# A recurrence stage re-divided between four engines and the transfer queues: |A|² and a running sum by accumulating transfers, one spectrum made twice, stores on another queue, a new order

## The chip, the cores and the metric

The kernel runs on one core of a Trainium2 chip. The metric is the device time of the whole program in microseconds (us), the median over runs. The core has a matrix engine (PE), a vector engine (DVE), a scalar engine (ACT), a general engine (POOL, GpSimd) and a queue engine (SP, SyncE). Each executes its own list of instructions strictly in order and waits at semaphores for the others. Transfers (DMA) are issued from SP (page queue q1) and from POOL (q0).

## The reference

Four layers on an image of 256×256 pixels with 128 channels. The change lies in layer 1 and at its seam to layer 2, so only layer 1 is shown (`x_ri` is the group-normalised image, 64 real and 64 imaginary channels; the result is added to the image).

```python
forget_gate = sigmoid(x_ri @ Wf + bf + 2.0)
input_gate = sigmoid(x_ri @ Wi + bi)
delta = softplus(x_ri @ Wd + bd) * 0.1
A_f = fft2 of the padded 7x7 kernels A (complex);  B_f likewise
mag = sqrt(Ar ** 2 + Ai ** 2 + 1e-08)
scale = 0.95 * sigmoid(mag) / (mag + 1e-08)
Ar, Ai = Ar * scale, Ai * scale
Bx_r, Bx_i = Br * x_r - Bi_ * x_i, Br * x_i + Bi_ * x_r
inp = delta * input_gate * Bx                 # real and imaginary part
# 16 times, from h = 0:
#   Ah = A * h (complex);  h_r = fg_r * Ah_r + inp_r;  h_i = fg_i * Ah_i + inp_i
```

Layer 2 begins with a group normalisation of the new image, so it needs that image's sum and sum of squares by channel. Layer 3 needs nine 128×128 products of its taps with a dense weight; they depend on no data.

## The kernel before

The program runs layer after layer; the image goes through DRAM between them (`x1T` into the recurrence, `x2T` out of it). `recurrence` (L864 to L1117) works on 64 blocks of 1024 pixels. A block's tiles hold 128 partitions (64 channels by two halves of the pixels) and, for each of real and imaginary, 512 numbers: a "wide" tile has 128×1024 numbers, a "thin" one 128×512. The 16 recurrence steps are done in closed form: with the 2×2 matrix of a step, its trace (tile `t`) and determinant (`d`), the 16th power is reached by repeated squaring.

The steps of a block are small functions of two or three letters (L994 to L1092), each one or a few instructions on one engine. The tuple `order` (L1095) lists each with a lag: in iteration `it`, step `(s, k)` works on block `it - k`, so five blocks are in flight. Everything is pinned to this order (`keep_in_program_order`), apart from the loads; so each engine's instructions follow the tuple, and each engine waits only where its next instruction does. There are 68 iterations (64 blocks and the largest lag, 4).

The steps that matter here, by engine:

- PE writes results into PSUM. `za`, `zb` are the spectra of A and B (14-row products of the tables `hs` and `ev`), `zd`, `zf`, `zi` the three gates, `bx` and `av` complex products by sums over identity-like matrices (L982), `m2` the sum |A|² of two squares, `pxb` a sum of three terms (step `xb`). The tiles tagged "z" (`za`, `zb` and the gates) share two PSUM buffers: a new one waits until the reader of the one before last is done.
- ACT: `a2` squares `za`, `zaa` copies both parts of `za` to the tile `ar` in SBUF; `lm`, `mg`, `lb`, `iv`, `sg` form the scale out of |A|²; `ab`, `ae`, `al_` belong to the softplus; `ig`, `f` are the gates' sigmoids; `tq*`, `dn*` squarings; `lD`, `eD` a reciprocal; `ev_` and `bn` (L1085, L1086) make the sum and the sum of squares of the result, with `accum_out` into `parts`. Changes between the logarithm's and the sigmoid's table are two table loads per iteration.
- DVE: products and sums of tiles: `s`, `fs_`, `ff`, `d_`, `D_`, `p0`, `p1` (spectrum B times image, tile `p`), `q`, `qg`, `v`, `tr*`, `u4`, `u8`, `xa`, `be`, `e_`, `al`, `y0`, `y1` (A's spectrum `ar` times `v`, tile `y`), `yf`, `yb`.
- POOL: `pf` (tile `fs`), `t`, `u2` (tile `u`), `t1` (tile `t` from `t,v`), and its queue: `ac1` and `ac2` add two results to the image tile `xc` by accumulating transfers (512 KB each), and `st` stores `xc` in two halves (L1091).
- SP: the loads of a block (`load`, L931): `xf` 512 KB, `xc` two of 256 KB, `hs` eight of 3.5 KB.

At the stage's end PE is kept warm (56 products), DVE reduces `parts`, and `triangle` (L1119) begins with `tap_products` (L1488: ten products of PE, four copies of DVE) and `group_affine` (L83), which reduces the statistics again, averages them by groups on PE, and forms scale and shift.

Of the kernel before, what the change touches and what calls it, by code (L numbers as in the profile page):

```python
# [9 lines left out]
F32 = mybir.dt.float32  # L10
# [21 lines left out]
class Kernel:  # L32
# [50 lines left out]
    def group_affine(self, pool, psum, stats, tag, shift=None, mv=None, busy=8):  # L83

        nc, V = self.nc, self.nc.vector
        pin = self.tc.keep_in_program_order
        pm = psum.tile([P, 2], F32, name=f"pm{tag}", tag="gn")
        d, v, mg, sd = (pool.tile([P, 1], F32, name=f"{n}{tag}") for n in ("gd", "gv", "mg", "sd"))
        if mv is None:
            mv = pool.tile([P, 2], F32, name=f"mv{tag}")  # L90
            V.tensor_reduce(mv, stats, AX.X, ALU.add)
            self.keep_busy(psum, busy)
            pin(self.mm(pm, self.g4n, mv))
            self.keep_busy(psum, 3)
            V.tensor_tensor(d, pm[:, 0:1], shift, ALU.add)
            V.scalar_tensor_tensor(v, d, d, pm[:, 1:2], ALU.mult, ALU.subtract)
            V.tensor_copy(mg, pm[:, 0:1])
            self.chain("table", self.act(sd, v, AF.Sqrt, bias=self.eps, scale=-1.0))
        else:
            self.keep_busy(psum, busy)  # L100
            pin(self.mm(pm[:, 0:1], self.g4, mv[:, 0:1]))
            self.keep_busy(psum, 3)
            V.tensor_copy(mg, pm[:, 0:1])
            V.tensor_sub(d, mv[:, 0:1], mg)
            V.scalar_tensor_tensor(v, d, d, mv[:, 1:2], ALU.mult, ALU.add)
            pv = psum.tile([P, 2], F32, name=f"pv{tag}", tag="gn")
            pin(self.mm(pv[:, 0:1], self.g4, v))
            self.keep_busy(psum, 3)
            self.chain("table", self.act(sd, pv[:, 0:1], AF.Sqrt, bias=self.eps))
        ab = pool.tile([P, 2], F32, name=f"ab{tag}")  # L110
        V.reciprocal(ab[:, 0:1], sd)  # L111
        V.scalar_tensor_tensor(ab[:, 1:2], mg, -1.0, ab[:, 0:1], ALU.mult, ALU.mult)
        return ab, mg, sd
# [750 lines left out]
    def recurrence(self, x1T, x2T, HD_, stats1, shift1, stats2, shift2):  # L864
# [7 lines left out]
        with ExitStack() as c:  # L872
# [40 lines left out]
            parts = wp.tile([P, 2, 2, NB], F32, name="parts2")  # L913
            shiftc = wp.tile([P, 2], F32, name="shiftc")
            V.tensor_copy(shiftc, abc[:, :, 1])
            fold = wp.tile([P, HC], F32, name="fold")
            V.tensor_tensor(fold, self.ident[:, :HC], self.ident[:, HC:], ADD)
            rows = lambda t: t.rearrange("p i (r v) -> p r i v", v=N)
# [5 lines left out]
            def act(out, in_, func, **kw):  # L924
                want = tables.get(func)
                if want not in (None, current[0]):
                    pin(nc.scalar.preload_act_table_set(want))
                    current[0] = want
                return pin(self.act(out, in_, func, **kw))

            def load(b):  # L931
                d = D[b]
                xf = d["xf"] = io.tile([P, 1024], F32, name="xf", bufs=2)
                nc.sync.dma_start(xf, x1T[:, b * 1024:(b + 1) * 1024])
                xc = d["xc"] = io.tile([P, 2, 512], F32, name="xc", bufs=6)
                for half in range(2):
                    src = x1T[:, b * 1024 + half * 512:b * 1024 + (half + 1) * 512]
                    nc.sync.dma_start(xc[half * HC:(half + 1) * HC], src.rearrange("(r c) n -> c r n", c=HC))
                d["hs"] = self.first_rows if b == 0 else self.row_transforms(io.tile([P, 2, HC], F32, name="hs", bufs=2), HD_, b)
# [3 lines left out]
            def wide(d, n, bufs=1):  # L943
                d[n] = tp.tile([P, 2, 512], F32, name=n, tag="w" + n, bufs=bufs)
                return d[n]
# [28 lines left out]
            def total(d, name, pairs):  # L974

                n = len(pairs)
                z = d[name] = ps.tile([P, n, 512], F32, name=name, tag="y" if n == 2 else "s", bufs=1 if n == 2 else 2)
                for i, terms in enumerate(pairs):
                    for k, (m, t) in enumerate(terms):
                        pin(self.mm(z[:, i], m, t, start=k == 0, stop=k == len(terms) - 1))  # L980
# [14 lines left out]
            def a2(d): act(rows(wide(d, "a2")), d["za"], AF.Square)  # L995
            def m2(d): total(d, "m2", [[(self.ident, d["a2"][:, 0]), (self.ident, d["a2"][:, 1])]])
            def lm(d): act(thin(d, "mag"), d["m2"][:, 0], AF.Ln, bias=1e-8)
# [5 lines left out]
            def ab(d): halves(d, wide(d, "az"), "d", "zd", AF.Identity)  # L1003
            def ae(d): act(wide(d, "ex"), d["az"], AF.Sigmoid, scale=-1.0)
            def al_(d): act(d["ex"], d["ex"], AF.Ln, bias=1e-37)
            def q(d): stt(wide(d, "q", 2), d["ex"], -1.0, d["az"], MUL, MAX)

            def sg(d): act(d["mag"], d["mag"], AF.Sigmoid)
            def s(d): tt(thin(d, "s", 3), d["mag"], d["inv"], MUL)
# [3 lines left out]
            def ig(d): halves(d, wide(d, "ig"), "i", "zi", AF.Sigmoid)  # L1013
            def zaa(d): act(wide(d, "ar", 2), d["za"].rearrange("p r i v -> p i r v"), AF.Copy)
# [3 lines left out]
            def t(d): gt(thin(d, "t", 3), d["fs"], d["ar"][:, 0], MUL)  # L1018
            def d_(d): tt(thin(d, "d"), d["m2"][:, 0], d["ff"], MUL)
# [20 lines left out]
            def dn2(d): squared(d, "dn2", "d", 2)  # L1040
            def tr2(d): stt(thin(d, "tr2"), d["d"], -2.0, d["tq2"], MUL, ADD)
            def u2(d): gt(thin(d, "u2", 2), d["t"], d["tr2"], MUL)
# [3 lines left out]
            def u4(d): tt(thin(d, "u4"), d["u2"], d["tr4"], MUL)  # L1046
            def tq8(d): squared(d, "tq8", "tr4")
            def dn8(d): squared(d, "dn8", "dn4", 2)
# [3 lines left out]
            def xa(d): stt(thin(d, "g", 2), d["t"], -2.0, d["u8"], ADD, MUL)  # L1052
# [13 lines left out]
            def y0(d): tt(wide(d, "y0"), d["ar"], both(d["v"][:, 0]), MUL)  # L1066
            def y1(d): tt(wide(d, "y1"), d["ar"], both(d["v"][:, 1]), MUL)
            def av(d): real_and_imaginary(d, "av", d["y0"], d["y1"])
            def yf(d): tt(wide(d, "yf", 2), d["av"], d["f"], MUL)
            def t1(d): (tt if last(d) else gt)(wide(d, "t1"), both(d["t"]), d["v"], MUL)  # L1070
# [14 lines left out]
            def ev_(d): statistic(d, 0, AF.Identity)  # L1085
            def bn(d): statistic(d, 1, AF.Square, shifted=True)  # L1086
            def st(d):
                b = d["b"]
                for half in range(2):
                    dst = x2T[:, b * 1024 + half * 512:b * 1024 + (half + 1) * 512]  # L1090
                    pin(nc.gpsimd.dma_start(dst.rearrange("(r c) n -> c r n", c=HC), d["xc"][half * HC:(half + 1) * HC]))  # L1091
            def ld(d): load(d["b"])  # L1092
# [3 lines left out]
                (e_, 3), (ld, 0), (za, 0), (u4, 2), (zb, 1), (a2, 0), (av, 2), (t, 1), (p1, 1), (zaa, 0), (m2, 0),  # L1096
                (tq8, 2), (al, 3), (zd, 0), (ev_, 4), (lD, 2), (q, 1), (yf, 2), (p0, 1), (tq2, 1), (dn2, 1), (tr2, 1),
                (eD, 2), (tr8, 2), (lm, 0), (dn8, 2), (mg, 0), (ab, 0), (t1, 3), (qg, 1), (lb, 0), (tq16, 2), (bx, 1),
                (ac1, 3), (iv, 0), (u8, 2), (yb, 3), (zf, 0), (sg, 0), (tq4, 1), (v, 1), (y1, 1), (f, 0), (xa, 2),
                (D_, 1), (s, 0), (u2, 1), (ac2, 3), (tr4, 1), (ae, 0), (fs_, 0), (zi, 0), (y0, 1), (ff, 0), (pf, 0),  # L1100
                (xb, 2), (ig, 0), (be, 2), (al_, 0), (bn, 4), (d_, 0), (dn4, 1), (st, 4),
            )
            deep = max(lag for _, lag in order)
            for it in range(NB + deep):
                for step, lag in order:
                    if 0 <= it - lag < NB:
                        D[it - lag]["b"] = it - lag
                        step(D[it - lag])
            warm = ps.tile([P, 1, 512], F32, name="warm", tag="s")
            for _ in range(56):  # L1110
                pin(self.mm(warm[:, 0, :P], self.ident, self.cmat))
            red = wp.tile([P, 2, 2], F32, name="partsum")
            V.tensor_reduce(red, parts, AX.X, ADD)
            pr = ps.tile([P, 2], F32, name="partps", tag="s")
            for ri in range(2):
                self.mm(pr[ri * HC:(ri + 1) * HC], fold, red[:, :, ri])
            V.tensor_copy(stats2[:, :, 0], pr)  # L1117

    def triangle(self, x2T, x3T, znT, prodD, rs2D, rs3D, stats2, shift2, stats3, shift3, prepare):  # L1119
# [12 lines left out]
        with ExitStack() as c:  # L1132
            wp = c.enter_context(self.pool(name="tw", bufs=1))
            with self.pool(name="twp", bufs=2, space=PSUM) as ps0:
                self.tap_products(ps0)
                ab, mg, _ = self.group_affine(wp, ps0, stats2, "2", shift=shift2, busy=0)
# [351 lines left out]
    def tap_products(self, ps):  # L1488

        W, V = self.weights, self.nc.vector  # L1490
        kt, wd = W["kt"], W["wd"]
        pb = ps.tile([P, 2], F32, name="cpb", tag="gn")
        self.mm(pb[:, 0:1], wd, W["bv"])
        V.tensor_copy(W["bw"], pb[:, 0:1])
        for t in range(3):
            pk = ps.tile([P, 3, P], F32, name="cpk")
            for n in range(3):
                self.mm(pk[:, n], kt[:, 3 * t + n, :], wd)
            V.tensor_copy(kt[:, 3 * t:3 * t + 3, :], pk)
# [178 lines left out]
    def run(self, ctx):  # L1678
# [10 lines left out]
        stats["2"] = const.tile([P, 2, 1], F32, name="stats2")  # L1689
        shift2 = const.tile([P, 1], F32, name="shift2")  # L1690
# [87 lines left out]
```

## Time and profile before

| what | value |
|---|---|
| median of 3 runs | 4687.53 us (4685.58 to 4689.0) |
| profiled execution, device time | 4687.51 us |
| its span, first to last instruction | 4685.7 us, granted PE clock 0.992 |
| recurrence: first `za` to the reduction of `parts` | 1654.5 to 2982.4 us |
| busy in 1700 to 2900 us | DVE 1192.3, ACT 1189.6, PE 1133.7, POOL 827.3 of 1200 us |
| DMA engines' share in the same stretch | 0.56 |
| first product of the next stage on the image (`mn`) | 2990.0 us |

The span is 1.8 us shorter than the device time. In the stage all compute engines are nearly always busy. An instruction's duration overlaps the next one's start by some 0.08 to 0.1 us on DVE and ACT, so sums of durations exceed the time; a step's price on its engine is the distance from its start to the next start. Busy time of PE is modelled, and POOL's includes time in which it holds an instruction that makes no progress.

### The profile page before, as it was taken

Reading aid. Unit: us, or ns where it says so; the run is one execution under the profiler, and the core shown is the slowest. Engines: PE = TensorE matmul, PEld = TensorE weight load, DVE = VectorE, ACT = ScalarE, POOL = GpSimd, SP = SyncE. Lnnn points to the kernel's source line nnn. Section 1 sums busy time; section 2 is a strip of 40 time slices with the busy share of each in tenths; the row PEclk is TensorE's granted clock in tenths of the full one; section 3 lists DMA queues with packets and bytes.
Section 4 is the critical chain, followed back from the end, with each engine's and each line's share of the span. In section 5 each row is a group of like instructions: output and inputs, shape, how many; then the busy total and the mean of one; then the engine's idle time right before and its main releaser. Section 6 shows DMA issues by size and latency. Waiting matters only on the chain. (4 is left out here: it accounts for less than half of the span.)

```text
span 4685.7 us, 79549 instructions
## 1 busy us (share of the span) xinstructions
PE 4524.4 (97%) x30447; PEld 2603.2 (56%) x30447; DVE 3753.2 (80%) x4828; ACT 3329.8 (71%) x5173; POOL 2099.7 (45%) x1364
## 2 busy tenths in 40 slices
PE   8999999999999989999999999899999999999999
PEld 2444555555555533333333333456999973379999
DVE  6776777777777779999999999787666677789885
ACT  6555888888888889999999999698443454442210
POOL 0343555555555547666667676333231245520000
PEclk9999999999999999999999999999999999999999
DMA  8894122222222235555555555576667668955432
GB/s 308 299 351 148 46 82 82 85 88 82 86 82 82 78 85 134 132 136 129 131 132 132 134 130 126 175 253 250 240 218 268 247 212 328 357 214 174 135 114 72
DMA packets 221045, 768.12 MB, mean 164 GB/s; under 512 B 58831, under 2 KB 62181, under 8 KB 180317
## 3 DMA queue, kind: packets, MB, share of 16 engines
q1 hardware_dynamic: 154550, 465.37, 29.2%
q0 software_dynamic: 64752, 297.22, 22.0%
q8 instruction: 244, 4.00, 0.3%
q14 instruction: 139, 1.13, 0.1%
q10 hardware_dynamic: 1360, 0.40, 0.0%
HBM read 431.26 MB, written 265.55 MB: 149 GB/s over the span
## 5 line engine op out<-in xcount | busy, mean ns | idle before, releaser
L586 DVE TENSOR_TENSOR e<-sc,bT 128x1024 f32<-128x1024 f32 x512 | 613.5, 1219 | 255.3 <-PE sc L61 254.2
L586 POOL TENSOR_TENSOR ks<-e 128x1024 f32<-128x1024 f32 x256 | 602.0, 2372 | 442.7 <-PE nd L61 429.3
L55 ACT ACTIVATE e<-e 128x1024 f32<-128x1024 f32 x512 | 539.4, 1054 | 39.2 <-DVE e L586 29.6
L61 PE MATMUL m<-U,v 128*128 128x128 f32 x4608 | 514.8, 275 | 1.5 <-DVE v L1613 1.5
L61 PEld LDWEIGHTS m<-U,v 128*128 128x128 f32 x4608 | 514.6, 192 | 1.6 <-DVE v L1613 1.6
L61 PEld LDWEIGHTS z<-wf,zt 128*128 128x128 f32 x4096 | 462.6, 192 | 54.2 <-DVE LR L1126 28.7
L61 PE MATMUL z<-wf,zt 128*128 128x128 f32 x4096 | 474.8, 277 | 6.2 <-DVE LR L1126 6.2
L1126 DVE TENSOR_TENSOR LR<-z,sg 128x512 f32<-128x512 f32 (+1 forms) x323 | 269.9, 866 | 165.4 <-ACT sg L55 165.4
L1126 POOL TENSOR_TENSOR zt<-zt,df 128x512 f32<-128x512 f32 x127 | 161.2, 1270 | 423.4 <-ACT df L55 423.4
L55 ACT ACTIVATE sg<-z 128x512 f32<-128x512 f32 (+1 forms) x323 | 160.7, 509 | 244.3 <-PE z L61 242.0
L61 PE MATMUL sc<-proj 32*128 32x256 f32 x4096 | 300.2, 404 | 2.9 <-DVE e L586 1.9
L955 POOL TENSOR_TENSOR fs<-f 128x512 f32<-128x512 f32 x64 | 174.5, 2727 | 273.7 <-DVE f L952 253.9
L61 PEld LDWEIGHTS sc<-proj 32*128 32x128 f32 x4096 | 188.4, 186 | 160.4 <-PE px L61 94.7
L61 PE MATMUL nd<-e,proj 128*32 128x256 f32 x4096 | 272.3, 384 | 2.6 <-DVE og L586 2.6
L55 ACT ACTIVATE dn<-dn 128x512 f32<-128x512 f32 x384 | 238.0, 620 | 10.2 <-DVE dn L586 6.1
L955 POOL TENSOR_TENSOR u<-t,tr 128x512 f32<-128x512 f32 x64 | 237.0, 3704 | 10.9 <-DVE tr L958 9.8
L955 POOL TENSOR_TENSOR t<-t,v 128x1024 f32<-128x1024 f32 x63 | 206.8, 3282 | 60.7 <-DVE t L952 60.7
L1653 ACT COPY m4s<-m 128x512 f32<-128x512 f32 x32 | 18.7, 585 | 301.4 <-PE m L61 301.4
L61 PE MATMUL z<-LR 128*128 128x256 f32 x1024 | 225.5, 384 | 7.5 <-DVE LR L1126 7.5
L1663 POOL DMA_DIRECT2D out_dram<-ys x32 | 36.9, 1155 | 420.3 <-DVE ys L1661 420.3
L61 PEld LDWEIGHTS z<-LR 128*128 128x128 f32 x1024 | 197.0, 193 | 35.1 <-DVE LR L1126 8.3
L1126 POOL TENSOR_TENSOR zt<-ga,zt 128x1024 f32<-128x1024 f32 x62 | 144.7, 2351 | 117.5 <-DVE ga L1126 117.5
(420 smaller groups left out, 10744.2 us busy)
## 6 DMA issues: line engine op xcount, KB each, us to landing
zt<-znT SPq DMA_DIRECT2D x96, 1024.0 KB
zt<-x2T SPq DMA_DIRECT2D x64, 1024.0 KB
xin<-in_x_dram SPq DMA_DIRECT2D x48, 1024.0 KB
xr<-x3T SPq DMA_DIRECT2D x46, 768.0 KB
x1T<-x POOLq DMA_DIRECT2D x64, 512.0 KB, 5.0
xf<-x1T SPq DMA_DIRECT2D x64, 512.0 KB
xc<-x1T SPq DMA_DIRECT2D x128, 256.0 KB
x2T<-xc POOLq DMA_DIRECT2D x128, 256.0 KB, 3.6
```

The lines of the kernel that those rows point to most:

```text
L55: return self.nc.scalar.activation(out, in_, func, bias=bias, scale=scale, **kw)
L61: return self.nc.tensor.matmul(out, lhsT, rhs, start=start, stop=stop)
L586: pin = lambda f: lambda *a, **k: tc.keep_in_program_order(f(*a, **k))
L955: pin(nc.gpsimd.tensor_tensor(out, a, b_, op))
L1126: pin = lambda f: lambda *a, **k: tc.keep_in_program_order(f(*a, **k))
L1653: nc.scalar.copy(m4, m[4])
L1663: nc.gpsimd.dma_start(out[row:row + 8].rearrange("r p t c -> p (r t) c"), ys.rearrange("p g k t c -> p (g k t) c"))
```

## The change

- `m2`: the two PE products are gone; an accumulating transfer on POOL's queue adds the second half of tile `a2` to the first (256 KB). Its readers, `lm` and `d_`, read `a2` in SBUF instead of PSUM.
- `ev_`: except for the last block, ACT's two passes with accumulation are gone; an accumulating transfer on POOL's queue adds `xc` to a tile `summed` (512 KB), which DVE reduces once at the end.
- `zaa` copies the real part alone. `y0`, `y1` read A's spectrum from PSUM, where a new step `zc` (lag 2, two products of PE) makes it again; it takes a "z" buffer, and `hs` gets three buffers.
- `u4` moves from DVE to POOL. `t1` of the last block moves from DVE to POOL.
- `st` moves from POOL's queue to SP's, pinned; in the program it stands between the fourth and the fifth `hs` load of the next block.
- The tuple `order` is new, and some tiles' buffer counts change.
- `tap_products` leaves `triangle` and is pinned at the head of iteration 2 of the recurrence, with its PSUM tiles under the tag "s" (two buffers).
- The group means are formed at the stage's end by products with `folded`; `group_affine` takes them as `means`.

```diff
-    def group_affine(self, pool, psum, stats, tag, shift=None, mv=None, busy=8):
+    def group_affine(self, pool, psum, stats, tag, shift=None, mv=None, busy=8, means=None):
...
+            else:
+                pm = means
...
+            V.memset(parts, 0.0)
+            summed = io.tile([P, 2, 512], F32, name="summed", bufs=1)
+            nc.gpsimd.memset(summed, 0.0)
...
+            folded = wp.tile([P, HC], F32, name="folded")
+            V.tensor_tensor(folded, self.g4n[:, :HC], self.g4n[:, HC:], ADD)
...
-            def m2(d): total(d, "m2", [[(self.ident, d["a2"][:, 0]), (self.ident, d["a2"][:, 1])]])
-            def lm(d): act(thin(d, "mag"), d["m2"][:, 0], AF.Ln, bias=1e-8)
+            def m2(d): pin(nc.gpsimd.dma_start(d["a2"][:, 0], d["a2"][:, 1], accum_op=ADD))
+            def lm(d): act(thin(d, "mag"), d["a2"][:, 0], AF.Ln, bias=1e-8)
...
-            def zaa(d): act(wide(d, "ar", 2), d["za"].rearrange("p r i v -> p i r v"), AF.Copy)
+            def zaa(d): act(thin(d, "ar", 2).rearrange("p (r v) -> p r v", v=N), d["za"][:, :, 0], AF.Copy)
...
-            def d_(d): tt(thin(d, "d"), d["m2"][:, 0], d["ff"], MUL)
+            def d_(d): tt(thin(d, "d"), d["a2"][:, 0], d["ff"], MUL)
...
-            def u4(d): tt(thin(d, "u4"), d["u2"], d["tr4"], MUL)
+            def u4(d): gt(thin(d, "u4"), d["u2"], d["tr4"], MUL)
...
-            def y0(d): tt(wide(d, "y0"), d["ar"], both(d["v"][:, 0]), MUL)
-            def y1(d): tt(wide(d, "y1"), d["ar"], both(d["v"][:, 1]), MUL)
+            def zc(d): spectrum(d, 0, "zc")
+            def turned(d, n, k):
+                v = d["v"][:, k].rearrange("p (r v) -> p r v", v=N).unsqueeze(2).to_broadcast([P, 2, 2, N])
+                tt(rows(wide(d, n)), d["zc"], v, MUL)
+            def y0(d): turned(d, "y0", 0)
+            def y1(d): turned(d, "y1", 1)
...
-            def t1(d): (tt if last(d) else gt)(wide(d, "t1"), both(d["t"]), d["v"], MUL)
+            def t1(d): gt(wide(d, "t1"), both(d["t"]), d["v"], MUL)
...
+                if last(d):
+                    statistic(d, 0, AF.Identity)
+                else:
+                    pin(nc.gpsimd.dma_start(summed, d["xc"], accum_op=ADD))
...
-                    pin(nc.gpsimd.dma_start(dst.rearrange("(r c) n -> c r n", c=HC), d["xc"][half * HC:(half + 1) * HC]))
+                    pin(nc.sync.dma_start(dst.rearrange("(r c) n -> c r n", c=HC), d["xc"][half * HC:(half + 1) * HC]))
...
+                (ld, 0), (za, 0), (a2, 0), (zc, 2), (m2, 0), (bx, 2), (zaa, 0), (ac2, 4), (u2, 2), (dn8, 3), (pf, 1),
+                (v, 2), (tq16, 3), (xb, 3), (t, 1), (tq4, 2), (y1, 2), (zd, 0), (ae, 1), (dn2, 2), (y0, 2), (lD, 2),
+                (ab, 0), (be, 3), (zb, 1), (ff, 1), (eD, 2), (av, 2), (tq2, 1), (lm, 0), (mg, 0), (e_, 3), (tr4, 2),
+                (al, 3), (zi, 0), (p0, 1), (dn4, 2), (lb, 0), (p1, 1), (al_, 1), (iv, 0), (u4, 2), (yf, 2), (ig, 0),
+                (t1, 3), (d_, 1), (tq8, 2), (yb, 3), (zf, 0), (tr2, 1), (q, 1), (f, 0), (tr8, 2), (qg, 1), (ac1, 3),
+                (u8, 2), (sg, 0), (s, 0), (D_, 1), (bn, 4), (xa, 2), (ev_, 4), (st, 4), (fs_, 0),
...
+                if it == 2:
+                    self.tap_products(ps)
...
+            V.tensor_reduce(parts[:, 0, :, 0:1], summed, AX.X, ADD)
```

## The prediction

> **What bounds the kernel now.** I read the busy times of the stage's middle first, then where one step, `v`, starts in each block, then each engine's timeline over one iteration, last the seam to the next stage.
>
> The windows view (columns: stretch, length, busy us and instructions of PE, weight load, DVE, ACT, POOL, then clock, DMA share, GB/s) shows DVE and ACT at 99%:
>
> ```profile
> 2000.00:2400.00 400.00, 378.34 (x1148) 132.76 (x1148) 396.51 (x495) 396.23 (x671) 270.68 (x159) 1.00 0.56 131
> ```
>
> The instructions around tile `bx` give the step `v`: count, shortest/median/longest ns, first and last start. 63 distances in 1268.6 us: 20.14 us per iteration.
>
> ```profile
> L958 DVE SCALAR_TENSOR_TENSOR v<-q,bx x64: 1204/1215/1222, 1684.1 to 2952.7; 128x1024 f32<-128x1024 f32 x64
> ```
>
> DVE's timeline (start, duration): two of three iterations take 19.65 us from `v` to `v`, which is DVE's own work; about each third takes 21.15. In the long ones `qg` lasts 2.31 instead of 1.22. Start to start, a 128x512 step costs 0.60 (112.29 to 112.89, leaving out the 2000), a 128x1024 one 1.14, two `p` 1.32.
>
> ```profile
> 2098.86 2.31 DVE L952 TENSOR_TENSOR q<-q,ig 128x1024 f32<-128x1024 f32 x1
> ...
> 2112.29 0.68 DVE L952 TENSOR_TENSOR u<-u,tr 128x512 f32<-128x512 f32 x1
> 2112.89 1.40 DVE L958 SCALAR_TENSOR_TENSOR p<-xc,abc,zb 128x512 f32<-128x512 f32 x2
> 2114.21 0.69 DVE L952 TENSOR_TENSOR t<-u,t 128x512 f32<-128x512 f32 x1
> ```
>
> POOL's timeline: the same 128x512 product takes 1.31 beside `p` and 4.49 beside a run of other DVE steps. Its 4.49 end 1.2 us after DVE turns to `v` at 2122.47, a step with one operand in PSUM. So POOL computes only while DVE reads PSUM: 1.22 to 1.3 us for 512 numbers, 2.33 for 1024. The transfer's distance to the next instruction, 0.63, is what issuing one costs.
>
> ```profile
> 2119.20 4.49 POOL L955 TENSOR_TENSOR u<-t,tr 128x512 f32<-128x512 f32 x1
> 2128.58 2.79 POOL L955 TENSOR_TENSOR fs<-f 128x512 f32<-128x512 f32 x1 [3.20 <-DVE f L952]
> 2132.61 1.31 POOL L955 TENSOR_TENSOR t<-fs,ar 128x512 f32<-128x512 f32 x1
> 2134.62 3.31 POOL L955 TENSOR_TENSOR t<-t,v 128x1024 f32<-128x1024 f32 x1 [0.70 <-DVE t L952]
> 2138.23 0.94 POOL L1077 DMA_DIRECT2D xc<-t  x1 [0.30 <-POOL t L955]
> 2138.86 4.48 POOL L955 TENSOR_TENSOR u<-t,tr 128x512 f32<-128x512 f32 x1
> ```
>
> PE's timeline; the distances are its prices: `pxb` 2.77, `zb` before `av` 1.13, `m2` 1.91, `zd` 1.87 (1.94 with its tail), `bx` 3.63.
>
> ```profile
> 2145.25 1.13 PE L61 MATMUL pxb<-g,ident 128*128 128x512 f32 x2
> ...
> 2148.02 1.13 PE L61 MATMUL za<-ev,hs 14*128 14x512 f32 x4
> 2148.94 1.20 PE L61 MATMUL zb<-ev,hs 14*128 14x512 f32 x4
> 2150.07 1.13 PE L61 MATMUL av<-y,ident 128*128 128x512 f32 x2
> ...
> 2154.29 1.98 PE L61 MATMUL m<-a,ident 128*128 128x512 f32 x4 [0.52 <-ACT a L55]
> 2156.20 1.94 PE L61 MATMUL zd<-xf,gwd 128*64 128x512 f32 x8
> 2158.07 1.13 PE L61 MATMUL bx<-p,scaledr 128*128 128x512 f32 x2
> ...
> 2161.70 1.94 PE L61 MATMUL zf<-xf,gwf 128*64 128x512 f32 x8
> ```
>
> **The parts, per iteration.** *DVE* loses `u4`, 0.60. `y0`, `y1` now read PSUM; `yf`, which does so already, costs 1.14 like them: 0, at worst 2 x (1.32 - 1.14) = 0.36 if they go like `p`. `d_` reads SBUF: 0.60 as before. DVE: 19.65 - 0.60 = 19.05 (to 19.41).
>
> *ACT* loses `ev_` (two of 0.63 and two reads of 0.19: 1.37 from its first start at 2115.26 to `D` at 2116.63) and half of `zaa` (0.91 to 0.52): 19.8 - 1.76 = 18.0. *PE* loses `m2`, 1.91, and gains `zc`, 1.13; `za` and `zb` (2169.17, both in 1.1) no longer overlap: about 19.0. *POOL* gains `u4` (1.25), two transfers to issue (0.63 each, the distance after `ac1`), loses two stores (1.30).
>
> *POOL's windows.* In DVE's new order PSUM readers stand together: `v`, `y1`, `y0`, `be` (4.02) and `p0`, `p1`, `yf` (3.8). POOL's queue puts `u2`, `pf`, `t` (3 x 1.25 = 3.75) before the first gap and `u4`, `t1` (1.25 + 2.33 = 3.58) in the second window. They fit, with 0.3 and 0.2 to spare, so I price `u4` on POOL at nothing. If a window is missed, a DVE step waits as `qg` does (1.1), or POOL waits as in the 4.49 row (3.2).
>
> [...]
>
> *A new ring of waits.* `zc` takes the "z" buffer of `zf` and waits until ACT has finished `f`. PE then goes `zc` 1.13, `bx` 3.63, `pxb` 2.77, `zd` 1.94 in order: 9.47, with two hand-overs (0.06, 0.08 as at the first `za`) 9.61. ACT's `ab` waits for `zd`, and from `ab` to the end of `f` ACT has (starts to starts): `ab` 1.14, six of 0.52 (`eD`, `tq2`, `lm`, `mg`, `dn4`, `lb`), 0.14 because `mg` directly follows `lm` that feeds it (0.66 in the `inv` pair at 1664.62), `al_` 0.97, `iv` 0.62, table 1.30, `ig` 1.13, `tq8` 0.52, `f` 1.25: 10.19. The ring is 9.61 + 10.19 = 19.80 us, and it must be gone round once per iteration. It exceeds DVE's 19.05 and ACT's 18.0. ACT idles at `ab`, 1.2 us, for it. So the period falls from 20.14 to 19.80, not to 19.05. [...] Bounds: 19.6 (without the 0.14 and the hand-overs) to 20.0.
>
> *Where the rest lies in it*, counted from the end of `f`: `sg`, `bn`, `a2` end at 0.4 + 1.55 + 1.0 = 3.0; `bx` ends at 4.8, so `v` starts at 4.9; `zd` ends at 9.5, `zb` and `av` (3.70) at 14.4, `zi` and `zf` (1.78, 1.94) at 18.1. DVE from `v`: 4.02, then `ff`, `e_`, `tr4`, `al` (2.4), `p0`, `p1` (2.64): 14.0, so `yf` waits 0.45 for `av`, and DVE's round is 19.5.
>
> *Transfers.* `m2` is issued at 3.1, and `lm`, with all of ACT behind it, wants it at 9.6 + 1.14 + 1.04 = 11.8. The nearest rows are accumulations of 512 KB: 4.4 to 7.2 us to landing, median 4.9. Half the bytes can't need more than 7.2, so 1.5 is left: cost 0, and no gain, since it sets no end. `ev_` (512 KB, same row) is waited for only by the next one and the end. A 512 KB accumulation keeps the DMA engines busy some 2.7 us (share near 1 from 2138 to 2142), so 4 us are added per 19.8: 0.56 becomes about 0.77. Behind `m2` on POOL stand `ac2` and `u2`; `ac2` goes out at 3.7, `u2` wants its window at 4.7. On SP the two stores (0.65 each) wait for `ac2` to land, and behind them stand four `hs` (0.83 each), then `xf` and `xc`. `za` of the next block needs those `hs`. PE reaches `za` at 18.1 and can bear 18.9 (19.8 less `za`'s 0.92). With 6.3 for `ac2` (4.9 and half a transfer of 2.7 in front), 3.7 + 6.3 + 1.3 + 3.3 = 14.6, and some 2.5 to land (below the least landing seen, 3.0 for 256 KB): 17.1. Covered, with 1.8 to spare.
>
> *Filling, draining, seam.* `v` of block 0 moves from iteration 1 to 2. I lay the steps on end with the durations of the first rows: `a2` ends at 1657.4, `m2` lands 4.9 later, then `lm`, `mg`, `lb`, `iv` (2.6), table 1.3, `ig`, `f`, `sg` (2.9): 1669.0. Second round: `a2`, `zaa`, `ae`, `ab` to 1672.6, `tq2` to 1675.1 (POOL's `pf` and `t` need 2.6 from `p0` at 1671.8), table, `lm` to `iv` (3.5 with `al_`), table, `ig`, `f`: 1683.5. So `zc` could start at 1683.6 and `v` at 1688.4, against 1684.07. But the taps' copies are pinned on DVE behind `fs_` (ends 1686.7), and with two "s" buffers the second and third group of products wait for copies: `za`, in order behind them, starts at about 1688.9, `v` at 1694.6. So the fill costs 10.5 us, 6.2 of it the taps; bounds 4 and 13. The first distance shrinks to about 17 (no `pxb`), from 18.0. Draining: after the last `v`, before, 29.2 us; now ACT has two passes less after DVE's end (3.0), but the chain `ac1`, `ac2`, `ev_` of block 62 (4.9 each) stands beside it: about 25.4. Seam: without taps and the second reduction `mn` could start 4.5 us earlier, but the 1 MB `zt` it reads is loaded from 2983.5 at 410 GB/s and can't be there before about 2988, so 2.0. The memsets and `folded` lie in idle time of POOL and DVE.
>
> Sum: last `v` at 1694.6 + 17 + 62 x 19.80 = 2939.2, 13.5 before the old 2952.7; draining -3.8; seam -2.0: **-19.3 us**. On the profiled execution's 4687.51, which the median (4687.53) matches, that is 4668.2.
>
> **The rivals.**
> 1. DVE sets the pace (the ring is shorter than its terms): DVE's round of 19.5: 62 x 0.3 less, 4649.6. For it: DVE is what bounds now; against: PE's and ACT's terms are plain rows. 0.12.
> 2. No change: POOL's windows slip in some iterations as now, 0.49 on average; the ring hides 0.2 of it in DVE's slack: period 20.1, 4687. For it: 0.2 to 0.3 us of room, and the same pattern in the old order; against: POOL reaches each window early. 0.17.
> 3. Slower: the stores on SP. If `ac2` needs over 8.1 us to land (18.9 less the terms above), each further us delays `za`, `zc` and so the period. With 9.3 the period is 21.0: 4668 + 62 x 1.2 = 4743; with 8.5, 4693. For it: the longest landing now is 7.2, and `m2` is put in front, `ev_` beside; against: the median leaves 1.8. 0.16.
>
> **How the numbers follow.** Forecast 0.55 (4655 to 4681 by the ring's bounds, with some 6 either way from the fill), rivals 0.12, 0.17, 0.16. The range, 4648 to 4700, leaves out most of rival 3 above (0.14) and little below (0.05). Of this kernel a measurement can tell about 0.2%, 9.4 us, from no change. Faster: 0.47 of the forecast and rival 1, 0.59; the same: 0.08 of the forecast and 0.12 of rival 2, 0.20; slower: the other 0.05 of rival 2 and rival 3, 0.21.
>
> **What would show it.** Right: `v` every 19.8 us without long iterations; ACT waiting about 1.2 us at `az` for `zd`; PE waiting at `zc` for `f`; `qg` always near 1.22; no wait at `mag` for the transfer. Wrong: DVE idle at `ff` or `qg` with POOL's `u` beside it (rival 2); `za` waiting for `hs`, SP waiting long for `xc<-yf` (rival 3); DVE without a wait at `v` (rival 1); in the fill, `v` of block 0 earlier than 1690.

## The result, and the profile after

The changed kernel takes 4787.17 us (median of 4 runs, 4785.01 to 4787.85) against 4688.26 for the kernel before on the same chip: a ratio of 1.0212, 95% interval 1.02 to 1.0225. It is 2% slower, some 99 us, where the prediction said 4668.2.

The profiled execution has a span of 4783.2 us (before 4685.7) and a granted PE clock of 0.964 (before 0.992). The windows view of the same stretch as before (length, then busy us and instructions of PE, weight load, DVE, ACT, POOL, then clock, DMA share, GB/s) shows where to look:

```profile
2000.00:2400.00 400.00, 383.62 (x1085) 133.20 (x1082) 357.03 (x451) 346.30 (x562) 208.75 (x166) 0.91 0.76 159
```

DVE and ACT, 99% busy before, are now busy for 89% and 87% of the time. PE is busy for longer with fewer instructions, and its granted clock is 0.91 instead of 1.00. The transfers' share rose to 0.76, as estimated (0.77).

The instructions around tile `bx` give `v` (count, shortest, median and longest ns, first and last start):

```profile
L966 DVE SCALAR_TENSOR_TENSOR v<-q,bx x64: 1207/1221/1223, 1699.4 to 3044.4; 128x1024 f32<-128x1024 f32 x64
```

63 distances in 1345.0 us are 21.35 us per round, against 20.14 before and 19.80 forecast. PE's timeline of one round and the start of the next (start, duration, product, count, and in brackets the idle time before it and what ended it) shows what a round holds:

```profile
2199.45 1.89 PE L61 MATMUL zf<-xf,gwf 128*64 128x512 f32 x8
2201.72 1.20 PE L61 MATMUL za<-ev,hs 14*128 14x512 f32 x4 [0.38 <-ACT ig L55]
2203.40 1.95 PE L61 MATMUL zc<-ev,hs 14*128 14x512 f32 x4 [0.48 <-ACT f L55]
2205.28 2.08 PE L61 MATMUL bx<-p,scaledr 128*128 128x512 f32 x2
2207.15 1.92 PE L61 MATMUL bx<-p,scaledn 128*128 128x512 f32 x2
2208.85 1.79 PE L61 MATMUL bx<-p,scaledi 128*128 128x512 f32 x2
2210.48 1.02 PE L61 MATMUL bx<-p,scaledr 128*128 128x512 f32 x2
2211.34 1.02 PE L61 MATMUL pxb<-g,ident 128*128 128x512 f32 x2
...
2224.61 1.20 PE L61 MATMUL za<-ev,hs 14*128 14x512 f32 x4 [0.39 <-ACT ig L55]
2226.28 1.13 PE L61 MATMUL zc<-ev,hs 14*128 14x512 f32 x4 [0.48 <-ACT f L55]
2227.34 1.98 PE L61 MATMUL bx<-p,scaledr 128*128 128x512 f32 x2
```

PE waits at `za` for `ig` and at `zc` for `f`, as the ring of waits says. But then the same products last almost twice as long: `zc` 1.95 instead of 1.13, a pair of `bx` 1.92 instead of 1.02, and then 1.02 again. `bx` takes 6.06 us here and 3.63 before. That is the clock at half. The trace has a record of the granted clock; in this round it falls to half at 2203.57 and is back at 2210.40. The windows view, cut at these times and in steps of 3.41 us (columns as above):

```profile
2200.16:2203.57 3.41, 2.55 (x12) 0.69 (x10) 3.41 (x5) 3.40 (x7) 0.72 (x1) 1.00 0.98 171
2203.57:2206.98 3.41, 3.41 (x6) 1.04 (x7) 3.41 (x6) 3.38 (x8) 0.37 (x1) 0.50 1.00 233
2206.98:2210.40 3.42, 3.42 (x5) 1.35 (x4) 0.88 (x1) 3.40 (x6) 2.48 (x4) 0.50 0.80 158
2210.40:2213.81 3.41, 3.41 (x9) 1.33 (x7) 2.16 (x2) 1.35 (x2) 2.63 (x3) 1.00 1.04 227
```

DVE and ACT pay for it:

```profile
2206.65 1.22 DVE L960 TENSOR_TENSOR f<-f,s 128x1024 f32<-128x1024 f32 x1
2211.61 1.22 DVE L966 SCALAR_TENSOR_TENSOR v<-q,bx 128x1024 f32<-128x1024 f32 x1 [3.75 <-PE bx L61]
2212.87 2.35 DVE L960 TENSOR_TENSOR y<-zc,v 128x1024 f32<-128x1024 f32 x2
```

The starts of `za` from 1836 to 2890 us are 19.53 us apart 6 times, 21.2 apart 28 times and 22.9 apart 15 times. By the record of the clock the 6 have no stretch at half clock, the 28 have one of 3.41 us and the 15 one of 6.83. So a round is 19.53 at full clock, 1.7 more with 3.41 us at half clock (half of it) and 3.35 more with 6.83. Had all rounds been of 19.53, the 63 distances would have taken 1230.4: the clock costs 114.6 us, more than the whole loss of 99.

### The profile page after: what moved, and what is told of

Its sections match the earlier page's. It is cut to its first block, busy times and chain, and to the rows that moved or that the text cites. A ratio compares the mean times of both kernels' runs of the same rounds, so it can differ in the third digit from the quotient of the medians.

```text
span 4783.2 us, 79487 instructions
## 1 busy us (share of the span) xinstructions
PE 4632.4 (97%) x30449; PEld 2633.6 (55%) x30449; DVE 3698.1 (77%) x4766; ACT 3234.8 (68%) x4921; POOL 1945.7 (41%) x1429
## 3 DMA queue, kind: packets, MB, share of 16 engines
q14 instruction: 138, 1.13, 0.1%
## 5 line engine op out<-in xcount | busy, mean ns | idle before, releaser
L55 ACT ACTIVATE dn<-dn 128x512 f32<-128x512 f32 x384 | 238.6, 621 | 10.1 <-DVE dn L589 6.0
L963 POOL TENSOR_TENSOR u<-u,tr 128x512 f32<-128x512 f32 x64 | 105.8, 1654 | 264.9 <-DVE tr L966 264.9
L1004 POOL DMA_DIRECT2D a<-a x64 | 54.6, 853 | 386.9 <-ACT a L55 386.9
L55 ACT ACTIVATE az<-zd,gbd 128x512 f32<-128x512 f32 x128 | 81.0, 684 | 183.5 <-PE zd L61 181.3
L966 DVE SCALAR_TENSOR_TENSOR v<-q,bx 128x1024 f32<-128x1024 f32 x64 | 78.1, 1221 | 151.6 <-PE bx L61 151.6
```

Source lines behind the costliest of these rows:

```text
L55: return self.nc.scalar.activation(out, in_, func, bias=bias, scale=scale, **kw)
L963: pin(nc.gpsimd.tensor_tensor(out, a, b_, op))
L966: pin(V.scalar_tensor_tensor(out, a, k, b_, op0, op1))
L1004: def m2(d): pin(nc.gpsimd.dma_start(d["a2"][:, 0], d["a2"][:, 1], accum_op=ADD))
```

## The experiments

The first theory: the new order puts two products of 14 rows, with a short wait before each, between the last gate and `bx`; PE does too little there, and its clock is halved. Rivals: the waits alone do it (a); the few rows alone do it (b); the taps' products or the fill start it (c). All times are medians, all ratios against the kernel before in the same batch. A period is the mean distance of `v`, as above.

### zc behind bx

```diff
-  (za, 0), (a2, 0), (zc, 2), (m2, 0), (bx, 2), (zaa, 0),
+  (za, 0), (a2, 0), (m2, 0), (bx, 2), (zc, 2), (zaa, 0),
```

> Only the step zc moves, from in front of bx to behind it; nothing else changes. Theory (the ring f, zc, bx, pxb, zd, ab, f sets the period, and PE's clock falls because PE waits between zf, za and zc, where it has only two 14-row products): the ring loses bx, PE has work while ACT does f, the granted clock in the stage returns from 0.91 to about 1.00, bx takes 3.6 instead of 5.2 us, v comes every 19.0 to 19.5 us instead of 21.35, time 4787 - 63 x 2.1 = about 4655 us (4640 to 4675). Rival (the clock falls for another reason, such as the heavier transfers or the higher load as a whole, which this leaves as it is): clock stays near 0.91, period 20.7 to 21.3, time above 4745 us.

Measured (run zc_late): 4644.6 us, ratio 0.9906 (0.9889 to 0.9922). One step moved by two places turns 2.1% slower into 0.9% faster. The windows view:

```profile
2000.00:2400.00 400.00, 391.95 (x1212) 134.17 (x1212) 397.81 (x501) 386.50 (x626) 236.59 (x189) 1.00 0.86 180
```

The clock is back at 1.00, `bx` at 3.63, and DVE is 99% busy. The transfers' share is higher still (0.86 against 0.76) at this clock, so the heavier transfers weren't what brought it down. The period is 19.15: under the ring's 19.53, because `bx` no longer stands behind `zc` and so no longer waits for `f`, and close to the 19.05 that the prediction worked out for DVE alone. PE's timeline has one stretch of 14 rows at a time, with a single wait:

```profile
2214.61 1.89 PE L61 MATMUL zf<-xf,gwf 128*64 128x512 f32 x8
2216.78 1.20 PE L61 MATMUL za<-ev,hs 14*128 14x512 f32 x4 [0.28 <-ACT ig L55]
2217.90 1.13 PE L61 MATMUL bx<-p,scaledr 128*128 128x512 f32 x2
```

This takes away the ring and the clock's fall together, so it doesn't say which part of the stretch matters.

### Filling the waits: 128 rows, or 14

The order stays as changed. Two products of 128 columns stand before `za` and two before `zc`.

```diff
+                for _ in range(2):
+                    pin(self.mm(fillers["w"][:, 0, :P], self.ident, self.cmat))
                 spectrum(d, 0, "za")
```

> As the changed kernel, with two 128x128 products of identity-like matrices (0.45 us) in front of za and two in front of zc, written to a PSUM tile that nobody reads; they fill PE's two waits of 0.4 to 0.5 us. The ring of waits stays. Theory (waits lower the clock, the ring sets the rest): clock back to about 1.00, v every 19.5 to 19.8 us without longer iterations, time about 4680 us (4665 to 4695). Rival 1 (something else lowers the clock): clock 0.91, time 4785 to 4800 us. Rival 2 (the waits are needed to hide hand-overs, fillers only delay zc): clock 1.00 but period over 20.3, time over 4715 us.

Measured (run fill_dense): 4721.02, ratio 1.0075 (1.0058 to 1.0091), clock 0.96 in the stage, period 20.37. This is 26 us over the upper end of what the theory wanted. Period and time are those of its rival 2, but the clock isn't at 1.00, and the rounds without loss take 19.74, as the theory had it: the miss lies in rounds that still lose clock.

In the other one the fillers have 14 rows, `ev[0:2*KS, 0:P]` and `ev[0:2*KS, P:2*P]`.

> The same fillers with 14 rows instead of 128 (a corner of the table ev times itself), of the same length. If PE's clock follows how long PE waits, this does what the dense fillers do: clock about 1.00, about 4680 us. If it follows how much of the array works, so that za and zc with 14 rows count little, the clock stays near 0.91 and the time within 20 us of the changed kernel's 4787.

Measured (run fill_thin): 4769.99, ratio 1.0181 (1.0164 to 1.0198), clock 0.91, period 21.06, as forecast for few rows. PE's timeline shows no idle time between `zf` and `bx`, and a slow `bx` (1.77, 1.92) all the same:

```profile
2220.38 1.89 PE L61 MATMUL zf<-xf,gwf 128*64 128x512 f32 x8
2222.19 0.71 PE L61 MATMUL filler<-ev 14*128 14x128 f32 x4
2222.74 1.10 PE L61 MATMUL za<-ev,hs 14*128 14x512 f32 x4
2223.61 0.60 PE L61 MATMUL filler<-ev 14*128 14x128 f32 x4
2224.32 1.13 PE L61 MATMUL zc<-ev,hs 14*128 14x512 f32 x4
2225.38 1.77 PE L61 MATMUL bx<-p,scaledr 128*128 128x512 f32 x2
2226.94 1.92 PE L61 MATMUL bx<-p,scaledn 128*128 128x512 f32 x2
```

The waits weren't needed here: behind some 3.2 us of 14-row products without a pause, `bx` is slow in 39 of the 50 rounds that start between 1836 and 2890 us (so rival (a) isn't the cause here). With dense fillers, 28 of 51 rounds of the stage take 19.7 to 19.8 and 23 take 21.4, so 2.1 us of 14-row work split by 0.65 us of dense work was still enough in part of the rounds.

### The taps back at the seam

`tap_products` stands in `triangle` again, unpinned, with its PSUM tiles under its old tags.

> The changed kernel with tap_products back at the head of the triangle stage, as before. Theory: the fill loses PE's 5.4 us of waiting for the copies behind fs_ and some 3 us of products, so v of block 0 starts some 6 to 8 us earlier; the seam gains about 2 to 4 us of products, which also keep PE at work there. Net 3 to 7 us faster: 4780 to 4784 us; the period of v is unchanged at 21.3. Rival (the fill was slow for other reasons): v of block 0 within 2 us of 1699.4 and the time 2 to 4 us longer than 4787.

Measured (run taps_back): 4779.48, ratio 1.0206 (1.0188 to 1.0225), clock 0.90 in the stage, period 21.43. `v` of block 0 comes at 1689.5, 9.9 us earlier than with the taps in the fill (the prediction had put their delay at 6.2), and the whole is 8 us shorter by the medians, which the two intervals don't tell apart. Rival (c) falls: the taps delay the first `v`, but don't start the fall of the clock.

### The same products over 128 rows

`za`, `zb`, `zc` contract over all 128 rows; the rows beyond the 14 hold zeros.

```diff
-  pin(self.mm(z[:, r].rearrange("p i v -> p (i v)"), d["hs"][o].rearrange("q h c -> q (h c)"), ev[o]))
+  pin(self.mm(z[:, r].rearrange("p i v -> p (i v)"), d["hs"].rearrange("q h c -> q (h c)"), evs[2 * n + r]))
```

> The changed kernel with its order and its waits as they are; only the spectra's products za, zb and zc contract over all 128 rows (the hs tiles are cleared outside the 14 rows, and four copies of the columns hold zeros there), so they do the same in the same number of instructions. If the clock falls because few rows of the array work for about 2.3 us twice per iteration, it stays at 0.98 to 1.00, bx goes back to 3.63, the distance of v to the ring's 19.5 to 19.7, and the time to 4787 - 63 x (21.35 - 19.6) = about 4677. If the two waits of 0.4 to 0.5 us do it, or if rows of zeros count as no work, the clock stays at 0.91 and the time at 4780 to 4790.

Measured (run rows128): 4729.81, ratio 1.0094 (1.0077 to 1.011). The clock is 1.00 throughout the stage, as the theory wanted, but the time is 53 us above it. The windows view shows why:

```profile
2000.00:2400.00 400.00, 399.98 (x1138) 153.38 (x1137) 375.08 (x469) 363.94 (x590) 220.11 (x177) 1.00 0.82 169
```

PE is busy all the time and sets a period of 20.38. A spectrum now takes 1.8 us instead of 1.05: the two 14-row halves lie at different rows of the array and had overlapped. With PE full, the waits are gone too, so this run alone doesn't separate (a) from (b). The next one does.

### 128 rows, with the waits

As the last, but half of `av`'s products are left out (its result lacks the other part's terms), so that PE has time to wait.

```diff
-  def av(d): real_and_imaginary(d, "av", d["y0"], d["y1"])
+  def av(d): total(d, "av", [[(self.ident, d["y0"][:, 0])], [(self.ident, d["y1"][:, 0])]])
```

> As rows128 (za, zb, zc over all 128 rows), but half of av's products are left out (av lacks the terms with the other part, so the result is another), so that PE has some 1.7 us less than rows128's 20.4 and has to wait for ig before za and for f before zc again, as in the changed kernel. If the waits of 0.4 to 0.9 us alone lower the clock, it is 0.90 to 0.96 in the stage and the time 4760 to 4810. If only few rows and waits together do, the clock stays at 0.98 to 1.00, v at 19.9 to 20.1, and the time is 4695 to 4712.

Measured (run dense_waits): 4719.68, ratio 1.006 (1.0043 to 1.0077), clock 1.00, period 20.13 (both by 8 us and 0.03 over the upper end of what few rows wanted, and far below the other). PE waits longer than in the changed kernel, in one piece, and loses nothing:

```profile
2220.92 1.89 PE L61 MATMUL zf<-xf,gwf 128*64 128x512 f32 x8
2224.25 1.98 PE L61 MATMUL za<-ev,hs 128*128 128x512 f32 x4 [1.44 <-ACT ig L55]
2226.07 1.88 PE L61 MATMUL zc<-ev,hs 128*128 128x512 f32 x4
2227.78 1.02 PE L61 MATMUL bx<-p,scaledr 128*128 128x512 f32 x2
```

No `bx` of the stage is slow. So products over 128 rows, zero but for 14, kept the clock at 1.00 here, and with them a wait of 1.44 us cost nothing. In the kernel before, though, half clock follows a wait of 1.96 us among dense products; the section on the prediction shows it.

### Few rows in the fast order

In the order of `zc` behind `bx`, two more products go behind `za`, of 14 rows or of 128. PE has 1.72 us more to do in both.

```diff
+                for _ in range(2):
+                    pin(self.mm(spare["z"][:, 0], d["hs"][0:2 * KS].rearrange("q h c -> q (h c)"), ev[0:2 * KS]))
```

> zc behind bx as in zc_late (full clock, period 19.15), and behind za two more products of 14 rows into a spare tile: about 1.72 us more on PE per iteration, so PE sets the period (19.15 + 1.72 = 20.87) and doesn't wait; the stretch with 14 rows is 1.13 + 1.72 = 2.85 us, as long as za, zc and their two waits in the changed kernel. If few rows alone lower the clock: 0.90 to 0.96 in the stage, iterations longer by 1.7, 4790 to 4860. If it takes waits: clock 0.99 to 1.00 and 4644.6 + 63 x 1.72 = about 4753, as late_dense.

> The same as late_thin, but the two more products contract over all 128 rows (the identity with a loaded tile): the same time on PE. Both theories: clock 0.99 to 1.00, period 20.87, about 4753. It is the measure for late_thin.

Measured: late_thin 4780.12, ratio 1.0191 (1.0174 to 1.0208), clock 0.98; late_dense 4759.72, ratio 1.0147 (1.013 to 1.0164), clock 1.00. The 14-row work lowered the clock in the good order too, but far less often than in the changed kernel, so neither forecast for late_thin holds: 12 of the 50 rounds between 1836 and 2890 us have a slow `bx`, and 14 in the whole stage. 14 times 1.7 is 23.8 us, near the 20.4 between the two medians. Two rounds one after the other, with the same products and the same wait of 0.39:

```profile
2277.96 1.20 PE L61 MATMUL za<-ev,hs 14*128 14x512 f32 x4 [0.39 <-ACT ig L55]
2278.92 1.88 PE L61 MATMUL spare<-ev,hs 14*128 14x512 f32 x4
2280.72 1.30 PE L61 MATMUL bx<-p,scaledr 128*128 128x512 f32 x2
2281.82 1.91 PE L61 MATMUL bx<-p,scaledn 128*128 128x512 f32 x2
...
2300.48 1.20 PE L61 MATMUL za<-ev,hs 14*128 14x512 f32 x4 [0.39 <-ACT ig L55]
2301.44 1.87 PE L61 MATMUL spare<-ev,hs 14*128 14x512 f32 x4
2303.24 1.12 PE L61 MATMUL bx<-p,scaledr 128*128 128x512 f32 x2
2304.21 1.02 PE L61 MATMUL bx<-p,scaledn 128*128 128x512 f32 x2
```

What tells them apart is when they start. In six lost rounds in a row `za` starts at 2277.96, 2383.77, 2489.58, 2595.39, 2701.20 and 2807.01: always 105.81 apart, which is 31 times 3.4133. The records of the clock have a step of that length: in the kernel before and in the changed kernel, half clock begins and ends on a grid of 3.4133 us that keeps its phase through the whole stage. In the changed kernel the 44 stretches between 1836 and 2897 us last one or two steps of it (3.41 or 6.83), and the start of the first (1838.34) and the end of the last (2896.48) are 310.00 steps apart. So in these traces the clock changes in windows of 3.4133 us that don't follow the rounds; the starts of late_thin fit rounds that are hit when their stretch lies badly in such windows.

The changed kernel's trace also shows what a bad window was there. Take those at full clock between 1830 and 2895 us, and in each the time that PE's records of dense products cover (64 rows or more). The 44 windows with 1.18 us or less are all followed by half clock, and of the 209 with 1.22 or more none is. Of the windows at half clock themselves, the 15 with 2.58 or less are followed by another, and the 43 with 2.77 or more are not. In rows128, dense_waits and late_dense the clock from 2000 to 2400 us is 1.00.

Write a start as its position in such a window: the start of `za` divided by 3.4133, the part behind the point. (It counts from the start of the span, not of a window; where the grid lies differs between traces, at 0.58 in the changed kernel and 0.85 in the kernel before.) The losses of late_thin start at 0.30 to 0.37; rounds at 0.93 to 0.27 are spared. Its undisturbed round of 20.82 us is 6.10 windows: the position drifts by 0.10, and a loss of half a window (1.7 us) throws it out of the bad part. The changed kernel's 19.53 is 5.72 windows; a loss of a half makes it 6.22, of a whole one 6.70. Its positions in one pattern of 150.1 us are 0.05 (spared), 0.77, 0.99, 0.69, 0.91, 0.61, 0.83 (all hit): each loss leads to a place that is hit again.

### The same order, paced otherwise

To test that, the changed kernel gets useless dense work before `zd`, inside the ring.

```diff
+                for n in (512, P):
+                    pin(self.mm(spare["z"][:, 0, :n], self.ident, d["xf"][:, :n]))
                 gate(d, "d")
```

> The changed kernel, and before zd two more dense products into a spare tile (512 and 128 columns): by PE's prices 0.86 + 0.21 = 1.07 us of work for nothing inside the ring, whose round goes from 19.53 to about 20.60 us at full clock. The changed kernel's pattern repeats after 150.1 us, 7 iterations: if the clock is judged in windows of a fixed 3.41 us, that is 44 of them; 19.53 is 5.72 windows, and each loss of half a window or a whole one throws the next round into the windows where it is lost again. 20.60 is 6.04 windows: the rounds drift by 0.04, and a loss of half a window should throw them out of the bad part for some ten rounds. Then about one iteration in 8 to 16 loses 1.7 us, and the time is 4787 - 63 x (21.35 - 20.75) = about 4750, in spite of the added work. If the stretch za, zc lowers the clock by itself in most iterations, whatever their period, the work is added: 4787 + 63 x 1.07 = about 4854.

Measured (run paced): 4781.9, ratio 1.0197 (1.018 to 1.0214), clock 0.97 in the stage. An undisturbed round takes 20.62, so 63 rounds have 69 us more to do, and yet the time is no longer than the changed kernel's (5 us shorter by the medians, which the intervals don't tell apart). Losing in most rounds whatever the period, which would have given 4854, is out. The size was missed by 32 us: ten or more rounds in a row are spared (positions 0.05 to 0.44), then the first loss, at 0.45 or 0.48, leads to 0.99 to 0.04, where two or three rounds lose a whole window each, before the next lands at 0.05. The bad part is wider than I had thought: rounds are hit at 0.45 to 0.48 and at 0.99 to 0.04, and none starts in between. Of 49 distances 35 are 20.6, 4 are 22.3 and 10 are 24.0.

### Single parts, and the fastest version

`u4` on DVE again, in the order with `zc` behind `bx` (`gt` becomes `tt`):

> zc behind bx, and u4 back on DVE. DVE was 397.8 of 400 us busy in zc_late, period 19.15. If DVE sets the period there, one step of 0.60 more per iteration gives 19.65 to 19.75 and 4644.6 + 63 x 0.5 to 0.6 = 4676 to 4682. If PE or ACT sets it (PE's products add up to the same 19.15), less than +10: 4645 to 4655.

Measured (run late_u4): 4676.36, ratio 0.9976 (0.9966 to 0.9986), period 19.67, DVE 397.91 of 400 us busy. Moving `u4` is worth 32 us; DVE sets the pace there, as the first forecast had it.

`ev_` on ACT again, in the same order (no `summed`):

> zc behind bx, and the result's sum back on ACT (two passes of 1.37 us together per block), no accumulating transfer into one tile. ACT was 386.5 of 400 us busy in zc_late, 18.5 us per iteration: with 1.37 more it is 19.87, over DVE's 19.05, and the time 4644.6 + 63 x 0.7 = about 4690. If the accumulating transfers themselves hold something up (DMA share 0.86), part of this comes back: 4650 to 4680.

Measured (run late_ev): 4690.79, ratio 1.0008 (0.9999 to 1.0018), period 19.96. The accumulating transfer is worth 46 us; that the DMA share falls from 0.86 to 0.67 without it brought nothing. ACT is 396.53 of 400 us busy, as expected, but DVE too (397.91), with fewer instructions: its `ff` lasts 1.57 on average instead of 0.68 (columns: busy us and mean ns, idle before).

```profile
L960 DVE TENSOR_TENSOR ff<-f 128x512 f32<-128x512 f32 x20 | 31.4, 1568 | 0.0
```

19.05 and 0.89 are 19.94, the period. A DVE step held up in this way is what the prediction's rival 2 described (as `qg` in the kernel before), so which of the two engines sets this pace isn't told apart.

The fastest: `zc` behind `bx`; the taps' products in iteration 0, before `s`; the last two blocks' sums by ACT; 100 instead of 56 products at the end.

```diff
+                    if it == 0 and step is s:
+                        self.tap_products(ps)
...
-                if last(d):
+                if d["b"] >= NB - 2:
                     statistic(d, 0, AF.Identity)
```

> zc behind bx as in zc_late (4644.6), the taps' products in iteration 0 where DVE waits, the sum's accumulation done by ACT for the last two blocks, and 100 instead of 56 products that fill the seam. Fill: v of block 0 about 6 to 10 us earlier than 1705.6; the last transfer no longer ends the drain: -3 to -4; PE at full clock at the seam: -1 to -2. 4630 to 4636. If the fill is set by ACT and the transfers alone, only the last two: 4640.

Measured (run best): 4636.08 (4635.57 to 4638.21), ratio 0.9892 (0.9876 to 0.9909): 51 us faster than before, 151 faster than the changed kernel. From the first `za` to `v` of block 0 it takes 36.6 us, 7.6 less than with the taps in iteration 2. The end brought nothing: from the last `v` to `mn` it is 36.2 us against 36.0, since `mn` now waits for its image, and it still lasts almost twice as long (1.93 for what took 1.07 in the kernel before):

```profile
2935.61 1.93 PE L61 MATMUL mn<-zt,tmeana 128*32 128x512 f32 x8 [1.11 <-DMA zt<-x2T]
```

## Why the prediction was wrong

**The step that failed** is the ring's sum. It priced `zc` at 1.13 and `bx` at 3.63, from rows of the old order, where PE's clock was at 1.00, and so took for granted that the new order keeps the clock. In the new order `bx` takes 4.9 to 6.5 us in most rounds, `zc` up to 1.95. By the record of the clock, 43 of 49 rounds run at half clock for 3.41 or 6.83 us. The ring itself was right, though priced a little too high: 19.53 at full clock against 19.80, and the paced order, with 1.07 us more put into it, has an undisturbed round of 20.62. The lower bound of 19.6 was a slip: 19.80 without the 0.14 and the two hand-overs (another 0.14) is 19.52. Over 63 rounds the clock adds 114.6 us, the ring's smaller size takes back 17. No rival had it either: the prediction looked for a new wait, a slower transfer or a closed window at POOL, and found PE's own two waits of the ring, but took them for harmless idle time.

**The hint** was in the profile of before: its drain has `pxb` at 2.07 and 1.59 after PE had waited for 3.23 us, and the record has the clock at half from 2955.43 to 2958.84. I read such lines as a cold start and end of the stage, not as a price that a new stretch of light work in the middle could bring.

```profile
2955.85 2.07 PE L61 MATMUL pxb<-g,ident 128*128 128x512 f32 x2 [3.23 <-DVE g L958]
2957.71 1.59 PE L61 MATMUL pxb<-dn,twice 128*128 128x512 f32 x2
2959.14 1.02 PE L61 MATMUL pxb<-tq,negid 128*128 128x512 f32 x2
```

There was one in the middle too, hidden by a mean clock of 1.00. In one round of the old stage `bx` takes 5.30 us, after a wait of 1.96 among dense products; the record has the clock at half from 2242.04 to 2245.45, and in the window before it dense products cover 1.46 us and nothing else runs. Four other windows of that stage have as little (1.43 to 1.44) with 14-row products (four times 14, side by side) in the other 1.98 us, and are spared.

```profile
2240.69 1.10 PE L61 MATMUL bx<-p,scaledr 128*128 128x512 f32 x2 [1.96 <-DVE p L958]
2241.63 1.49 PE L61 MATMUL bx<-p,scaledn 128*128 128x512 f32 x2
2242.91 1.91 PE L61 MATMUL bx<-p,scaledi 128*128 128x512 f32 x2
```

**The fill** was sized at +10.5 and is +15.3 (`v` of block 0 at 1699.4, forecast 1694.6). The path was right: the third `za` was expected at 1688.9 and starts at 1689.29 behind the taps, after PE had waited 5.41 for the copy of `bwc`. From there to `v` it takes 10.1 instead of 5.7, with `za`, `zc` and `bx` at half clock (the record has it at half from 1684.74 to 1698.40): the same fault.

**The drain and the seam** were to gain 5.8. From the last `v` to the end of the span it is 1738.8 against 1733.0 before: 5.8 lost, 11.6 off. The accumulations were priced at 4.9 us from issue to landing each; they have medians of 4.7 (`t`), 7.1 (`yf`) and 8.3 (`summed`), so the reduction waits for the last one: the term for the chain `ac1`, `ac2`, `ev_` was too small. PE idles 10.90 us, and the first products of the next stage run at half clock (the record has it at half from 3070.56 to 3094.45):

```profile
3074.79 1.22 DVE L1130 TENSOR_REDUCE parts<-summed 128x2 f32<-128x1024 f32 x1 [6.10 <-DMA summed<-xc]
```
```profile
3076.94 0.38 PE L61 MATMUL partps<-partsum,folded 128*64 128x2 f32 x4 [10.90 <-DVE partsum L1132]
...
3082.76 1.94 PE L61 MATMUL mn<-zt,tmeana 128*32 128x512 f32 x8 [0.25 <-DVE twbe L1185]
```

The two together: the last `v` 105.2 late and the rest 11.6 make the 116.8 us by which the span exceeds the one forecast (4783.2 against 4668.2 less the 1.8 that lie around the span).

**What held.** DVE's work: 19.15 in the order that lets it run, against 19.05. `u4` on POOL at nothing, or nearly: it takes 1.66 (1.25 in the sum), `t1` 2.38 (2.33), and in the changed kernel `ff` never lasts longer than 0.68. In zc_late it is held up to 1.65 in some rounds (0.75 on average), but without the move 32 us are lost. That POOL computes only while DVE reads PSUM was too strong a reading: in the old order's round with `qg` at 2.31 POOL's `u` runs in the same time, 2098.43 to 2100.08, and it is DVE that is held. `y0` and `y1` from PSUM at nothing (two in 2.35). `m2`'s transfer in time (median 3.3 us to landing, no wait at `mag`). The stores on SP (rival 3): SP's queue never held up `za`, even with the period at 19.15. And rival 1, DVE's pace, is what `zc` behind `bx` brings: 4644.6 against its 4649.6, but in another order than the one for which it was stated.

## What to carry to other kernels

A product's price on PE holds only for the clock at which it was taken: `zc` was priced at 1.13 and took up to 1.95 here. When an order puts products of few rows, or waits, side by side, look whether any other stretch of the profile has such a pair, and price what follows it at half clock too. A mean clock of 1.00 over a stage can hide a single loss, as it did in the kernel before (3.41 us). In the changed kernel it was enough to count the dense products: after 1.18 us of them or less in a window of 3.41 at full clock, the next window ran at half clock, and after 1.22 or more it didn't. It paid here to put dense products on both sides of a spectrum of 14 rows: that was two places in a tuple, and 143 us, some 24 of them from the shorter period that DVE then sets. If rounds of a loop come in a few lengths that differ by a fixed amount, compare their starts with that amount before looking for a wait.

## What the runs showed of the hardware

- In the traces of the kernel before and of the changed kernel, half clock (0.50) comes in whole steps of 3.4133 us, one or two at a time in the middle of the stage, on a grid that keeps its phase (in the changed kernel over 310 steps). What came ahead of it differs: in the changed kernel gaps of 0.38 and 0.48 us around products of 14 rows; in the kernel before one gap of 1.96 us among dense products. With fillers of 14 rows and no gap at all the clock was 0.91 (fill_thin).
- Light work: some 1.1 us of 14-row products with a wait of up to 0.39 us left no `bx` slow between 1836 and 2890 us in zc_late, and `za` and `zb` side by side (2.05 us, at four places of the array) are followed by no loss in the kernel before. Over 128 rows, zero but for 14, the same products kept the clock at 1.00 (rows128, dense_waits). In the changed kernel, half clock followed all full-clock windows of 3.41 us with 1.18 us of dense work or less and none with 1.22 or more; the one loss in the middle of the kernel before comes at 1.46 with nothing beside it. How products of few rows or few columns bear on it stays open.
- How often a loop was hit went with its period: 88% of the rounds at 19.53 us (the changed kernel), 24% at 20.82 with a stretch that is no shorter (late_thin). Adding 69 us of useless work made the changed kernel no slower (paced: ratio 1.0197 against 1.0212).
- A spectrum's two products of 14 rows, at different rows of the array, overlapped: four instructions in 1.05 us (`zc` to `pxb` in zc_late), against 1.8 over all 128 rows (rows128).
